# A graph layer on one core: counts of a block made in pairs of pairs, and five searches of the opening moved back

## The chip, the cores and the metric

The kernel runs on one core of a Trainium2 chip. The metric is the device time of one execution in microseconds, as the median of the runs shown. The profile is of one further execution, whose own time stands beside its span below.

## The reference

A layer of a graph network over 6250 nodes with 64 features and 206,250 edges. The edges are sorted by their destination; half of the random edges are the other half reversed, and each node has a loop to itself.

```
h   = relu(layernorm(x))                        # 6250 x 64
msg = h[src] + edge_attr_64                     # 206250 x 64
agg = segment_sum(msg, dst)                     # 6250 x 64
out = x + relu(agg @ W1 + b1) @ W2 + b2         # hidden width 128
```

So each node sums over its edges the normalized features of the sources and the features of the edges, and two small dense layers follow.

## The kernel before

**Two sums.** The edge features are loaded in chunks of 42 nodes (SyncE's queue) and summed by TensorE with a one-hot matrix of the destinations, into a PSUM tile `bank` (`chunk_sum`, L517). The source features aren't gathered for most edges. Instead the kernel counts, for each destination, how often each source occurs, and multiplies the counts with the normalized features: sources are written as 49 rows h of 128, edges stand in tiles of 127 for 3 destinations each, and a tile's counts are one fp8 matmul of two one-hot matrices (`count`, L971; `hotb`, made by VectorE at L958). `count(n)` is called for odd steps n and makes 12 tiles (one pair of steps) in a PSUM tile `pc` of two buffers. ScalarE copies it into the SBUF `ring` (L981). For the last pair of a block that copy has two parts, the first 12 rows h ahead of the other 37. `products` (L994) then multiplies, for h = 0 to 48, the features of h with the ring's counts of a whole block of 252 nodes, into the PSUM tile `pv`.

**Blocks and steps.** There are 23 blocks (0 to 22) of 14 steps; a step is 6 tiles, so a block has 7 pairs, called below by their odd steps 1, 3, ... 13. The products of block b - 1 are run inside block b: 12, 12, 12 and 13 rows h at steps 1, 3, 5 and 7, each behind that step's count (`PART`, L86 and L1315). The ring holds 22 steps, so that the first 8 steps of block b have room beside the block before.

**What else stands in a block's order.** Feature sums at steps 9 and 11 (two and four of a block's six chunks, 48 and 96 matmuls as the trace counts them), the placing of the block before's feature sums into `pv` (L549) at step 3, at most two sums of an edge group (`sum_group`, L580, copied by ScalarE at L582) at steps 3 and 5, the first dense layer `ph` (L1072) at step 10 with its relu on ScalarE (L1074), the second `po` (L1080) at step 13, and the turning of the next edge keys (`pk`, L771, copied at L791 and L799). In blocks 7 to 14 a check `over` (`inside_rel`, L906) runs on ScalarE at step 8, ahead of that step's other work. `ph`, `po`, `over` and the values of the turned keys use one PSUM tile of one buffer, tag `po`.

**Who sets the order.** The order of the instructions of each engine is that of the program text. The loop over the steps (L1305) calls, for step n: what stands in `tops` and `before`, the count, the one-hot rows, the encoding of keys, the products, what stands in `later`, `turns` and `behind`. The lists `before` and `behind` are written by hand by step (L1182, L1205). GpSimd issues all indirect gathers, each at L360. The gathers of source rows for the last 17 edge groups go through a list `queue`, which `pool_until` works off by a clock of estimated costs; `room` limits how many gathers may be issued until a later step sets it again (L1105 to L1118).

**The opening.** Each of 15 rows of lists (row i covers 128 windows of 3 nodes) begins at an edge that has to be searched: `fetch_row(i)` gathers 256 destinations for each window on GpSimd, `seek(i)` counts on ScalarE with an accumulator how many are smaller (L383), and `place` turns this into an edge number on VectorE (L388, L390). The words of the lists are gathered at these numbers (`fetch_pair`). Also here, `chunk_starts` and `chunk_columns` work out where the feature chunks start, `fetch_dst(t)` gathers the destinations of 32 chunks (`dstq`), and the node features are normalized and split in two fp32r halves (L634, L638). Windows with more than 127 edges, at most 14, need a second list: `second_ends` to `second_nodes` find them (`pnext` at L831, ranks at L844 to L846, picks at L855 to L868) at the steps in `SECOND` (L84), ScalarE's and VectorE's parts by `before`, TensorE's by `behind`.

```
for n in range(NSTEP):
    b, s = block_of(n)
    for f in tops.get(n, []) + before.get(n, []):
        f()
    if n % 2:
        count(n)
    ...
    if b and 1 <= s < FRESH:
        products(b - 1, PART[s], PART[s + 1])
    ...
    for f in later.pop(n, []) + turns.pop(n, []) + behind.get(n, []):
        f()
    pair_ends(n)
```

Of the kernel before, what the change touches and what calls it, by code (L numbers as in the profile page):

```python
# [53 lines left out]
GA = G - GP  # L54
# [13 lines left out]
NW = 23  # L68
SB = 3
ST = 6  # L70
STEPS = BT // ST
# [9 lines left out]
UPPERS = (5, 7, 9)  # L81
LOWERS = (11, 15, 17)
CLEARS = (61, 47, 33, 19, 18)
SECOND = (7, 8, 9, 10, 11, 13, 14, 20, 22)  # L84
FIRST = 12
PART = (0, 0, 12, 12, 24, 24, 36, 36, HI)  # L86
CHUNKS = ((9, 9), (11, 11), (11, 11))
# [20 lines left out]
IC = -(-NWIN // P)  # L108
# [26 lines left out]
ROWS = 3  # L135
# [9 lines left out]
LAND_US = 4.0  # L145
NEED_P = N - 31 * GP - 6
OPENING_US = 8.0


def four_bytes(byte):  # L150
# [4 lines left out]
def gnn_kernel(ctx: ExitStack, tc: tile.TileContext, x, src_t, dst_t, dst_g, edge, w1, b1, w2, b2, out):  # L155
# [16 lines left out]
    def block_of(n):  # L172
        b = min(n // STEPS, NW - 1)
        return b, n - b * STEPS
# [200 lines left out]
    def fetch_row(i):  # L375
        at = rows_at + i * L1 if i < 11 else squares_at + (i - 11) * L1
        rows_of[i] = agg[:, at:at + L1].bitcast(I32)
        gather(rows_of[i], dst_g.rearrange("q h (r k) -> (q h r) k", k=L1), row_i[:, i:i + 1])

    def seek(i0, n):  # L380
        for i in range(i0, i0 + n):

            nc.scalar.activation(agg[:, junk_at:junk_at + L1 // 2].bitcast(BF16), rows_of[i], AF.Sign,  # L383
                                 bias=nhalf[:, i:i + 1], accum_out=first[:, i, 1:2])

    def place(i0, n):
        to = first[:, i0:i0 + n, 0]
        nc.vector.scalar_tensor_tensor(to, first[:, i0:i0 + n, 1], -0.5, middle[:, i0:i0 + n],  # L388
                                       op0=OP.mult, op1=OP.add)
        nc.vector.tensor_tensor(first_i[:, i0:i0 + n], to, limit[:, i0:i0 + n], op=OP.min)  # L390
# [56 lines left out]
    def fetch_dst(t):  # L447
        dsts[t] = late.tile([P, CQ], I32, tag="dstq", bufs=2, name="dstq")
        gather(dsts[t], dst_g.rearrange("q h (k o) -> (q h k) o", o=1), cols_i[:, t:t + 1])

    def chunk_nodes(t):

        dst = dsts.pop(t)
        relq = dst.bitcast(F32)
        nc.vector.tensor_scalar(relq, dst, cols[:, NT:], float(CN * RC * t), op0=OP.subtract, op1=OP.subtract)
        nc.vector.scalar_tensor_tensor(relq, iota_q, cols[:, t:t + 1], relq, op0=OP.subtract, op1=OP.max)
        known["n", t] = relq
# [94 lines left out]
    def tiles_of(g):  # L552
        return J if g < G - 1 else JL
# [56 lines left out]
    def norm_var(k):  # L610
        h0, h1 = thirds[k]
        nc.vector.tensor_reduce(var[:, h0:h1], squares.pop(k), AX.X, OP.add)  # L612
# [100 lines left out]
    def fetch_words(i0, n, p, index):  # L713
        words_of[i0] = late.tile([P, 2, P], I32, name="words", bufs=2)
        for i in range(n):
            gather(words_of[i0][:p, i, :], packed_1[:, :] if i0 < 4 else packed[:, :], index[i])

    def fetch_pair(i0):
        n = min(2, IC - i0)
        fetch_words(i0, n, P, [first_i[:, i:i + 1] for i in range(i0, i0 + n)])  # L720
# [166 lines left out]

    def second_fetch():
        queue.insert(0, (WORDS_US / 2, lambda: fetch_words(2 * PC, 1, NX, [flags.pop("i")[:, :]])))

    RP = 4
    bad = small.tile([P, 2 + 2 * RP], F32, name="bad")
# [202 lines left out]
    def fetch_h(g):  # L1095
        if g not in parts_of:
            load_h(g)
        for j in range(tiles_of(g)):
            queue.append((GATHER_US, lambda j=j: gather(
                parts_of[g][:, j, :], table[:, :], src_p[:, (g - GA) * J + j:(g - GA) * J + j + 1], OP.add)))  # L1100
        queue.append((0.0, lambda: fetched.setdefault(g, pool[0])))

    fetched = {}

    room = [1 << 30]  # L1105

    def pool_until(us):
        while queue and pool[0] <= us and (room[0] > 0 or not queue[0][0]):
# [16 lines left out]
            fetch_h(g + ROWS)  # L1125

    fetch_pair(0)
    for i in range(5, 11):
        fetch_row(i)
    seek(2, 1)  # L1130
    norm_var(0)
    for i in range(11, IC):
        fetch_row(i)
    src_turn(1)
    norm_var(1)
    firstp = small.tile([1, GP], F32, name="firstp")
# [24 lines left out]
    encode(0)  # L1161
    chunk_index(0, 2)
    fetch_dst(0)
    fetch_pair(2)
    fetch_dst(1)
    seek(7, 3)
# [4 lines left out]
    for q in range(2):  # L1171
        key_copies(1, q, columns(1))
    value_powers(1, columns(1))
    seek(10, 1)
    rows_of_tiles(1)
    load(0)
    for k in range(1, 3):
# [4 lines left out]
    load(2)  # L1182

    before = {
        2: [lambda: [fetch_h(g) for g in range(GA, GA + ROWS)], lambda: seek(11, 2)],
        5: [lambda: chunk_nodes(0), lambda: seek(13, 2)],
        6: [lambda: chunk_turn(0)],
        7: [lambda: place(7, 8)],
        18: [find_groups],
        87: [lambda: chunk_starts(2 * RC, NC)],  # L1190
        89: [lambda: chunk_rows(2 * RC, NC)],
# [10 lines left out]
    for n in range(2 * RP):  # L1202
        before.setdefault(106 + 14 * n, []).append(lambda n=n: inside_rel(n))

    behind = {}  # L1205
    for k in range(3):
        behind.setdefault(UPPERS[k], []).append(lambda k=k: split_upper(k))
        before.setdefault(LOWERS[k], []).append(lambda k=k: split_lower(k))
    for n, f in zip(SECOND, (second_ends, second_flags, second_ranks, second_picks, second_words, second_found, second_fetch, second_turn, second_nodes)):
        (behind if f in (second_ends, second_ranks, second_words, second_turn) else before).setdefault(n, []).append(f)  # L1210
# [24 lines left out]
    for i in range(2, IC):  # L1235
        c0, c1 = columns(i)[0][2], columns(i)[-1][2] + columns(i)[-1][1] - columns(i)[-1][0]
        n = min((n for n in range(deadline(c0) + 1 - TURN[-1][0]) if n % STEPS in (TURNS if i > 2 else (6,)) and c1 - R <= encoded(n)),
                key=lambda n: (i > 2 and TURNS.index(n % STEPS), -n))
# [4 lines left out]
            unpack_later(steps, lambda i=i: unpack_pair(i))  # L1243
        assert n <= (NW - 1) * STEPS + 7
        turn_later(n, i, P, columns(i))
    n = 27
    assert n + TURN[-1][0] <= deadline(SX)
    unpack_later([n - k for k in (4, 3, 2, 1)], lambda: unpack(2 * PC, 1, NX, second_b, NX))
    turn_later(n, 2 * PC, NX, [(0, NX, SX)])
    for t in range(1, NT):  # L1250
        n = 78 + 14 * t
        before.setdefault(n, []).append(lambda t=t: t > 1 and queue.insert(0, (GATHER_US, lambda: fetch_dst(t))))
        n = 49 if t == 1 else 86 + 14 * t
# [7 lines left out]
    for g in range(len(kept)):  # L1261
        n = 40 + 4 * g if g < 2 else 94 if kept[g][2] == 2 else XB * g * STEPS + 10
# [14 lines left out]
    for b in range(NW):  # L1277
        n = b * STEPS
# [23 lines left out]
        at_step(n, f)  # L1302

    assert len(PART) == FRESH + 1
    for n in range(NSTEP):  # L1305
        b, s = block_of(n)
        for f in tops.get(n, []) + before.get(n, []):
            f()
        if n % 2:
            count(n)  # L1310
        if n % (HT // ST) == 0:
            rows_of_tiles(n // (HT // ST) + 1)
        if n % (EB // ST) == AHEAD and n // (EB // ST) * EB + EB < TILES:
            encode(n // (EB // ST) + 1)
        if b and 1 <= s < FRESH:  # L1315
            products(b - 1, PART[s], PART[s + 1])
        if b and s == FRESH:
            add_products(b - 1)
            if b - 1 > SB:
                ready.append(b - 1)  # L1320
        if n in SECONDS:
            k = SECONDS.index(n)
            add_seconds(2 * k)
            if 2 * k + 2 >= NX:
                ready[:0] = range(SB + 1)
        if s in LAYERS and ready:
            mlp(ready.pop(0), n, LAYERS[s])
        for f in later.pop(n, []) + turns.pop(n, []) + behind.get(n, []):
            f()
        pair_ends(n)  # L1330
        if n >= 3:
            if s in (GROUPS if b < NW - 1 else LAST_GROUPS) and h_next < G and fetched.get(h_next, 1e9) + LAND_US <= clock(n + 2):
                group_hot(h_next)
                at_step(n + 2, features_h, h_next)
                h_next += 1
                add_later(n + 5)
            if n == 3:
                pool[0] = clock(n - 1) + OPENING_US
            pool_until(clock(n) + LAND_US)
# [5 lines left out]
    b = NW - 1  # L1345
# [161 lines left out]
```

## Time and profile before

| | before |
|---|---|
| median of 3 runs | 396.49 us (396.26 to 398.42) |
| the profiled execution | 396.92 us |
| its span, first to last instruction | 394.9 us |
| TensorE busy (matmul / weight load) | 335.2 us, 85% / 305.5 us, 77% |
| ScalarE busy | 327.0 us, 83% |
| VectorE busy | 307.5 us, 78% |
| GpSimd busy | 271.3 us, 69% |
| mean granted clock of TensorE | 0.995 of full speed |
| product runs (L994) | 1127 matmuls, 154.5 us |
| counts (L971) | 1932 matmuls, 78.3 us |
| copies into the ring (L981) | 184, 262.0 us |

The table is read so: no engine is busy all the time, and four are busy for more than two thirds of it, so a busy share alone doesn't say which one is waited for. That is read from the chain of waits and from the order of the instructions on TensorE and ScalarE in single blocks. TensorE's instructions overlap (a matmul's end is modelled), so the starts are the firmer numbers.

### The profile page before, as it was taken

To read this page: it belongs to the slowest core of one execution; us is meant where nothing else is said; L and a number is where in the kernel's file an instruction comes from. 1 tells how busy PE (TensorE), PEld (TensorE's weight loads), DVE (VectorE), ACT (ScalarE), POOL (GpSimd) and SP (SyncE) were. 2 spreads that over 40 slices of the span, in tenths; PEclk is the share of its full clock that TensorE was granted. 3 is DMA by queue.
4 is the path that set the end of the run, shared out by engine and by line. 5 is a ranking of instruction groups with operands and counts; after the bars stand their busy time and mean duration, and the time that the engine had idled before them with its cause. 6 is when DMAs were issued, how large, how long until landed. Compare 5 with 4: busy or idle time off the path is not lost.

```text
span 394.9 us, 17220 instructions
## 1 busy us (share of the span) xinstructions
PE 335.2 (85%) x7303; PEld 305.5 (77%) x7304; DVE 307.5 (78%) x804; ACT 327.0 (83%) x380; POOL 271.3 (69%) x204
## 2 busy tenths in 40 slices
PE   2053498889989989989899799989999999999993
PEld 1032387879878979979799799979889889988983
DVE  5965799989996977858886878978886878696631
ACT  7673979799989778978898989988889889987750
POOL 7774688877876885758767676767765876676400
PEclk9999999999999999999999999999999999999997
DMA  8967975869795785967868769967968976787500
GB/s 174 266 225 233 298 195 130 240 176 230 181 266 124 204 208 129 275 186 180 235 167 230 214 154 229 257 172 176 260 149 223 254 204 150 204 219 188 150 11 24
DMA packets 111947, 76.89 MB, mean 195 GB/s; under 512 B 30855, under 2 KB 107775, under 8 KB 111865
## 3 DMA queue, kind: packets, MB, share of 16 engines
q1 hardware_dynamic: 91134, 67.20, 57.0%
q0 software_dynamic: 20560, 8.28, 15.9%
q8 instruction: 59, 0.97, 1.0%
q10 hardware_dynamic: 171, 0.26, 0.2%
q14 instruction: 23, 0.19, 0.2%
HBM read 71.45 MB, written 4.26 MB: 192 GB/s over the span
## 4 chain that ended last, share of the span: by engine, by line
PE 71%; ACT 12%; DVE 6%; issue 5%; another core or an unknown queue 2%; DMA 1%; POOL 0%; DVEq 0%; ACTq 0%; SPq 0%; POOLq 0%
PE pv L994 31%; PE bank L517 13%; PE pc L971 13%; ACT ring L981 8%; PE ph L1072 3%; PE po L1080 3%; PE pv L549 3%; PE bank L580 2%; PE pk L771 2%; DMA xl<-in_x 1%; ACT sums L643 1%; DVE sums L601 1%; DVE sums L612 1%; ACT kq L791 1%
## 5 line engine op out<-in xcount | busy, mean ns | idle before, releaser
L981 ACT ACTIVATE ring<-pc 128x1764 fp32r<-128x1764 uint8 (+3 forms) x184 | 262.0, 1476 | 28.1 <-PE pc L971 18.0
L360 POOL DMA_INDIRECT pfeat<-table,src_p x132 | 226.2, 1713 | 78.2 <-PE bank L517 43.8
L994 PE MATMUL pv<-ring,h 128*128 128x252 f32 x1127 | 154.5, 286 | 10.2 <-ACT ring L981 9.0
L994 PEld LDWEIGHTS pv<-ring,h 128*128 128x128 f32 x1127 | 137.2, 188 | 12.5 <-ACT ring L981 10.6
L958 DVE TENSOR_TENSOR hotb<-at,of 127x576 int32<-127x576 bf16 x216 | 120.1, 599 | 2.0 <-PE pc L971 0.8
L971 PE MATMUL pc<-hotb 128*128 128x49 fp8e5 x1932 | 78.3, 186 | 4.3 <-issue 2.1
L971 PEld LDWEIGHTS <-hotb 128*128 128x128 fp8e5 x1932 | 67.7, 98 | 14.6 <-issue 4.2
L517 PE MATMUL bank<-feat,hotf 128*18 128x64 f32 x3288 | 64.5, 222 | 3.5 <-issue 2.8
L517 PEld LDWEIGHTS bank<-feat,hotf 128*18 128x18 f32 x3288 | 51.6, 99 | 10.1 <-issue 7.2
L504 DVE TENSOR_TENSOR hotf<-rel,iota 128x432 f32<-128x432 bf16 x69 | 41.5, 601 | 5.9 <-PE ph L1072 2.0
L1029 DVE TENSOR_TENSOR sums<-sums,pv 128x252 f32<-128x252 f32 (+2 forms) x27 | 8.1, 328 | 24.4 <-PE pv L994 19.3
L941 DVE TENSOR_TENSOR at<-iota_a,kq 128x576 bf16<-128x576 bf16 (+1 forms) x54 | 24.2, 448 | 0.4
L791 ACT ACTIVATE kq<-pk 128x512 bf16<-128x512 f32 (+18 forms) x48 | 17.9, 458 | 6.5 <-remote 5.0
L360 POOL DMA_INDIRECT words<-packed,first_i x15 | 17.1, 1143 | 5.6 <-issue 4.0
L947 DVE TENSOR_TENSOR of<-of,kv 128x288 bf16<-128x288 bf16 (+1 forms) x54 | 16.6, 308 | 2.6 <-ACT kv L799 0.2
L1072 PE MATMUL ph<-sums,w1s 128*128 128x252 f32 (+2 forms) x48 | 16.1, 416 | 2.9 <-ACT over L906 1.5
L360 POOL DMA_INDIRECT sums<-in_dst_g,row_i x15 | 15.0, 1001 | 4.8 <-issue 4.3
L306 PE MATMUL psrc<-shift,src 128*64 128x128 f32 (+1 forms) x16 | 4.1, 433 | 16.8 <-ACT src L303 16.8
L941 DVE TENSOR_TENSOR of<-iota_w,kq 128x288 bf16<-128x288 bf16 (+1 forms) x54 | 16.2, 300 | 0.6 <-ACT kq L791 0.6
L306 PEld LDWEIGHTS psrc<-shift,src 128*64 128x64 f32 (+1 forms) x16 | 3.1, 243 | 16.7 <-ACT src L303 12.1
L1080 PE MATMUL po<-w2s,after 128*126 128x64 f32 (+2 forms) x96 | 15.2, 280 | 0.0
L527 DVE COPY after<-bank 128x384 f32<-128x384 f32 (+1 forms) x23 | 12.7, 551 | 2.7 <-PE pc L971 2.7
(190 smaller groups left out, 300.5 us busy)
## 6 DMA issues: line engine op xcount, KB each, us to landing
feat<-in_edge SPq DMA_DIRECT2D x137, 384.0 KB
pfeat<-in_edge SPq DMA_DIRECT2D x16, 256.0 KB
pfeat<-table,src_p POOLq DMA_INDIRECT x132
xl<-in_x SPq DMA_DIRECT2D x3, 512.0 KB
out_y<-after SPq DMA_DIRECT2D x22, 63.0 KB
table<-xl SPq DMA_DIRECT2D x2, 512.0 KB
after<-in_x SPq DMA_DIRECT2D x4, 252.0 KB
table<-xl SPq DMA_DIRECT2D x1, 544.0 KB
```

The costliest lines, as they stand in the source:

```text
L360: ins = nc.gpsimd.indirect_dma_start(out=rows, out_offset=None, in_=source, in_offset=bass.IndirectOffsetOnAxis(ap=index, axis=0), compute ...
L504: nc.vector.tensor_tensor(hot_of[u][:, :n].rearrange("p c j w -> p (c j) w"), rel[:, c:c + n].rearrange("p c q k -> p (c q k)").unsqueeze( ...
L517: ins = nc.tensor.matmul(bank[q * QP:q * QP + WQ, at:at + D], hot_of[u][:, c, j, :], feats[u][c][:, j, :], start=(k == 0), stop=(k == JP - 1))
L791: nc.scalar.activation(kq[:, q, at:at + n].rearrange("s i k o -> s (i k) o"), pk[:, q, a:a + n].rearrange("s i k -> s (i k)").unsqueeze(2) ...
L941: nc.vector.tensor_tensor(to[:, :n].rearrange("s i k (m o) -> s (i k) m o", o=2), iota_k.rearrange("s (m o) -> s m o", o=2).unsqueeze(1).t ...
L947: nc.vector.tensor_tensor(pairs_of, pairs_of, kv[:, c:c + n].rearrange("s i k o -> s (i k) o").unsqueeze(2) .to_broadcast([P, 2 * n, WE // ...
L958: nc.vector.tensor_tensor(hot[:SLOTS, :n, c:c + m * A8].rearrange("s i (w a) -> s i w a", a=A8), at[:SLOTS, o:o + n, k].unsqueeze(2).to_br ...
L971: nc.tensor.matmul(pc[:, j * WPC:j * WPC + HI], hot[:, :P], hot[:, P:P + HI], start=True, stop=True)
L981: done.append(nc.scalar.activation(to[:, h:z, :mid - u], of[:, h:z, u:mid, :V], AF.Copy))
L994: nc.tensor.matmul(pvs[b], h2[:, h, :], ring[:, h, c:c + columns_of_block(b)], start=(h == 0), stop=(h == HI - 1))
L1072: nc.tensor.matmul(ph[:, :n], w1s, agg[:, start[b]:start[b + 1]], start=True, stop=True)
L1080: nc.tensor.matmul(po[:pairs[b], k, :], hid[:, k:2 * pairs[b]:2], w2s, start=True, stop=True)
```

## The change

Three things. First, in blocks 1 to 21 the counts of pairs 1 and 3 are both made at step 3, those of 5 and 7 at step 7, those of 9 and 11 at step 11, and that of 13 at 13 (`counted_at`); in the first and the last block each stays at its own step. Second, `fetch_row` of 10 to 14 goes on GpSimd behind `fetch_dst(0)`; `seek` of 10 to 14 goes behind steps 5 to 9, one each; `place(7, 8)` goes from step 7 to step 10, and the steps of the second lists' search in `SECOND` follow, with the unpacking and turning of the second lists' words from step 27 to 28. Third, `room` starts at 5 and not without a limit; `second_fetch`, at step 14, lifts the limit.

```diff
@@ -81,7 +81,7 @@
 UPPERS = (5, 7, 9)
 LOWERS = (11, 15, 17)
 CLEARS = (61, 47, 33, 19, 18)
-SECOND = (7, 8, 9, 10, 11, 13, 14, 20, 22)
+SECOND = (10, 11, 11, 12, 12, 14, 14, 20, 22)
 FIRST = 12
 PART = (0, 0, 12, 12, 24, 24, 36, 36, HI)
 CHUNKS = ((9, 9), (11, 11), (11, 11))
@@ -145,6 +145,7 @@
 LAND_US = 4.0
 NEED_P = N - 31 * GP - 6
 OPENING_US = 8.0
+OPENING = 5
 
 
 def four_bytes(byte):
@@ -887,6 +888,7 @@
 
     def second_fetch():
         queue.insert(0, (WORDS_US / 2, lambda: fetch_words(2 * PC, 1, NX, [flags.pop("i")[:, :]])))
+        room[0] = 1 << 30
 
     RP = 4
     bad = small.tile([P, 2 + 2 * RP], F32, name="bad")
@@ -1102,7 +1104,7 @@
 
     fetched = {}
 
-    room = [1 << 30]
+    room = [OPENING]
 
     def pool_until(us):
         while queue and pool[0] <= us and (room[0] > 0 or not queue[0][0]):
@@ -1125,12 +1127,10 @@
             fetch_h(g + ROWS)
 
     fetch_pair(0)
-    for i in range(5, 11):
+    for i in range(5, 10):
         fetch_row(i)
     seek(2, 1)
     norm_var(0)
-    for i in range(11, IC):
-        fetch_row(i)
     src_turn(1)
     norm_var(1)
     firstp = small.tile([1, GP], F32, name="firstp")
@@ -1161,6 +1161,8 @@
     encode(0)
     chunk_index(0, 2)
     fetch_dst(0)
+    for i in range(10, IC):
+        fetch_row(i)
     fetch_pair(2)
     fetch_dst(1)
     seek(7, 3)
@@ -1171,7 +1173,6 @@
     for q in range(2):
         key_copies(1, q, columns(1))
     value_powers(1, columns(1))
-    seek(10, 1)
     rows_of_tiles(1)
     load(0)
     for k in range(1, 3):
@@ -1182,10 +1183,10 @@
     load(2)
 
     before = {
-        2: [lambda: [fetch_h(g) for g in range(GA, GA + ROWS)], lambda: seek(11, 2)],
-        5: [lambda: chunk_nodes(0), lambda: seek(13, 2)],
+        2: [lambda: [fetch_h(g) for g in range(GA, GA + ROWS)]],
+        5: [lambda: chunk_nodes(0)],
         6: [lambda: chunk_turn(0)],
-        7: [lambda: place(7, 8)],
+        10: [lambda: place(7, 8)],
         18: [find_groups],
         87: [lambda: chunk_starts(2 * RC, NC)],
         89: [lambda: chunk_rows(2 * RC, NC)],
@@ -1202,7 +1203,7 @@
     for n in range(2 * RP):
         before.setdefault(106 + 14 * n, []).append(lambda n=n: inside_rel(n))
 
-    behind = {}
+    behind = {n: [lambda i=n + 5: seek(i, 1)] for n in range(5, 10)}
     for k in range(3):
         behind.setdefault(UPPERS[k], []).append(lambda k=k: split_upper(k))
         before.setdefault(LOWERS[k], []).append(lambda k=k: split_lower(k))
@@ -1243,7 +1244,7 @@
             unpack_later(steps, lambda i=i: unpack_pair(i))
         assert n <= (NW - 1) * STEPS + 7
         turn_later(n, i, P, columns(i))
-    n = 27
+    n = 28
     assert n + TURN[-1][0] <= deadline(SX)
     unpack_later([n - k for k in (4, 3, 2, 1)], lambda: unpack(2 * PC, 1, NX, second_b, NX))
     turn_later(n, 2 * PC, NX, [(0, NX, SX)])
@@ -1302,12 +1303,19 @@
         at_step(n, f)
 
     assert len(PART) == FRESH + 1
+    def counted_at(n):
+        b, s = block_of(n)
+        if not 0 < b < NW - 1:
+            return [n] if n % 2 else []
+        return {3: [n - 2, n], 7: [n - 2, n], 11: [n - 2, n], 13: [n]}.get(s, [])
+
+    assert STEPS == 14
     for n in range(NSTEP):
         b, s = block_of(n)
         for f in tops.get(n, []) + before.get(n, []):
             f()
-        if n % 2:
-            count(n)
+        for k in counted_at(n):
+            count(k)
         if n % (HT // ST) == 0:
             rows_of_tiles(n // (HT // ST) + 1)
         if n % (EB // ST) == AHEAD and n // (EB // ST) * EB + EB < TILES:
```

## Rows read from the trace of the kernel before

**Rows 1.** The page's fourth part: the chain that ended last, its shares by engine.

```profile
PE 71%; ACT 12%; DVE 6%; issue 5%; another core or an unknown queue 2%; DMA 1%; POOL 0%; DVEq 0%; ACTq 0%; SPq 0%; POOLq 0%
```

**Rows 2.** Timeline, TensorE, 306.5 to 323: start, us, instructions xcount [idle before <-releaser].

```profile
308.44 1.66 PE L994 MATMUL pv<-ring,h 128*128 128x252 f32 x12 [0.88 <-ACT ring L981]
309.94 0.47 PE L971 MATMUL pc<-hotb 128*128 128x49 fp8e5 x12
...
317.78 0.69 PE L1072 MATMUL ph<-sums,w1s 128*128 128x252 f32 x2
...
322.65 0.61 PE L994 MATMUL pv<-ring,h 128*128 128x252 f32 x3 [0.16 <-issue]
```

**Rows 3.** Timeline, TensorE, three narrow windows behind 310.2, which part a run.

```profile
310.26 0.47 PE L994 MATMUL pv<-ring,h 128*128 128x252 f32 x2
...
310.46 0.51 PE L994 MATMUL pv<-ring,h 128*128 128x252 f32 x3
...
310.57 0.40 PE L994 MATMUL pv<-ring,h 128*128 128x252 f32 x2
```

**Rows 4.** Timeline, ScalarE, 304 to 324.

```profile
319.65 1.63 ACT L981 ACTIVATE ring<-pc 128x1764 fp32r<-128x1764 uint8 x1
322.06 1.71 ACT L981 ACTIVATE ring<-pc 128x432 fp32r<-128x432 uint8 x2 [0.78 <-PE po L1080]
```

**Rows 5.** Timeline, TensorE, 223.5 to 238.

```profile
223.65 1.66 PE L994 MATMUL pv<-ring,h 128*128 128x252 f32 x12 [0.66 <-ACT ring L981]
...
229.40 0.47 PE L971 MATMUL pc<-hotb 128*128 128x49 fp8e5 x12
...
232.52 0.69 PE L1072 MATMUL ph<-sums,w1s 128*128 128x252 f32 x2
```

**Rows 6.** Timeline, ScalarE, 222 to 239.

```profile
228.32 3.24 ACT L981 ACTIVATE ring<-pc 128x1764 fp32r<-128x1764 uint8 x2 [0.49 <-PE pc L971]
231.45 0.60 ACT L906 ACTIVATE over<-rel,edge_w 128x411 f32<-128x411 bf16 x1
231.98 0.19 ACT L906 ACTIVATION_READ_ACCUMULATOR over<-rel,edge_w 128x1 f32 x1
...
234.33 1.63 ACT L981 ACTIVATE ring<-pc 128x1764 fp32r<-128x1764 uint8 x1
```

**Rows 7.** Instructions of line L1072 (ph): its engine idle until (us, times).

```profile
  ACT over L906: 3.9, 6
```

**Rows 8.** Timeline, ScalarE, 24 to 60.

```profile
39.55 0.50 ACT L383 ACTIVATE sums<-sums,nhalf 128x256 bf16<-128x256 int32 x1
...
40.18 0.51 ACT L383 ACTIVATE sums<-sums,nhalf 128x256 bf16<-128x256 int32 x1
...
50.24 1.10 ACT L634 ACTIVATE h<-xl 128x1088 fp32r<-128x1088 f32 x1
```

**Rows 9.** Timeline, TensorE, 24 to 72.

```profile
47.16 0.58 PE L831 MATMUL pnext<-ends,shift 128*128 128x15 f32 x2 [1.23 <-DVE ends L829]
...
48.59 1.48 PE L517 MATMUL bank<-feat,hotf 128*18 128x64 f32 x48
...
55.16 1.67 PE L994 MATMUL pv<-ring,h 128*128 128x252 f32 x12 [0.65 <-ACT ring L981]
```

**Rows 10.** Timeline, GpSimd, 14 to 64.

```profile
30.52 0.95 POOL L360 DMA_INDIRECT sums<-in_dst_g,row_i  x1 [0.30 <-issue]
...
36.30 1.35 POOL L360 DMA_INDIRECT dstq<-in_dst_g,cols_i  x1 [4.83 <-DVE cols L442]
```

**Rows 11.** Windows: us, busy us of PE, PEld, DVE, ACT, POOL; clock, DMA share, GB/s.

```profile
27.00:32.00 5.00, 0.33 (x2) 0.00 (x0) 0.00 (x0) 1.48 (x6) 3.55 (x4) 1.00 1.00 360
```

**Rows 12.** Timeline, VectorE, 25 to 52.

```profile
33.52 0.21 DVE L414 TENSOR_SCALAR starts<-pstart 1x64 f32<-1x64 f32 x1 [6.64 <-remote]
...
46.84 0.17 DVE L829 TENSOR_SCALAR ends<-first 128x15 f32<-128x15 f32 x1
```

**Rows 13.** All waits: engine, what waited <- for what: us in total, times, longest.

```profile
PEld bank L517 <- issue: 7.2, 23, 0.6
```

## The prediction, made before the changed kernel was run

> **What bounds the kernel now.** I read the page first, for the chain that ended last. 71% of it is TensorE and 12% ScalarE [rows 1]: TensorE sets the pace, and ScalarE, which copies each pair's counts from PSUM into the ring, stands between two of its pieces. Then the timeline of TensorE over one block late in the run, from the first product run (h 0 to 11 of the block before) at 308.44 us to the next at 322.65, a period of 14.21 us [rows 2]. What to see there: TensorE works without a break except in front of that first run, which waits 0.88 us for ScalarE's copy. Third, ScalarE in the same block [rows 4]: it has idle time, 0.78 us of it in front of the first part of the last pair's copy (322.06), which starts 4.28 us behind the MLP's ph (317.78) and releases the product run 0.59 us later. So one block is TensorE's work, plus one trip over ScalarE, whose slack is under 1 us. Fourth, a block in the middle, from 223.65 [rows 5, 6]: a check copy named over runs on ScalarE behind the copy of the fourth pair and shares a PSUM tile with ph; 6 idle times of ph's weight load or matmul, 3.9 us together, were ended by it [rows 7]; there are 8 such blocks (7 to 14). Last the opening up to 55.16 us, where the first product run starts [rows 8 to 12].
>
> **The counts, plain blocks.** I call a pair by its odd step. Counts 1, 5 and 9 move behind 3, 7 and 11; nothing is added or taken away. A count run takes 0.32 us (309.94 to 310.26) [rows 2, 3]. Behind it a product run's second matmul comes 0.20 us after the first (310.26 to 310.46), the next 0.11 after that (310.57) [rows 3]: a switch from counts to products costs 0.09 us. Up to ph: count 1, which filled the wait in front of the first run and so cost nothing, now costs 0.32 beside count 3; joining 5 and 7 saves a switch, 0.09; count 9 leaves, 0.32 + 0.09. Sum -0.18 us: ph comes earlier. Behind ph it is worse. Copy 11 starts 1.87 us behind ph in this block (319.65) [rows 2, 4] and 1.81 in the other (232.52 to 234.33) [rows 5, 6]; with the change copy 9 stands there and copy 11 comes behind it. Two copies in a row take 3.24 us (228.32) [rows 6], so one is 1.6 or a little less, 1.52 with the overlap. The last pair's copy starts at 1.75 + 1.52 + 1.52 = 4.79 us behind ph, where 4.28 is now: +0.51. Net +0.33 us a block, 13 blocks, +4.3 us. Bounds: -0.18 (ScalarE's slack larger than this block shows) and +0.5.
>
> One rule speaks against pairs here. The wait in front of the product run repeats in nearly every block, and its releaser is ScalarE's copy, a datum and not a free buffer [rows 2]. The Trainium skill (Perfetto Trace Analysis, Optimization Strategy) says that a gap which repeats on the saturated engine can mean too little PSUM for the next tile. By that rule a pair, which takes both count buffers, would wait as well. The trace does not yet bear it out: it is a rival below.
>
> **The blocks with the check copy.** Counts 5 and 7 now both follow the third product run, which ended at 229.40 [rows 5]; count 1 adds 0.32 before it, count 5 takes 0.32 and a switch away, so it ends at about 229.3, count 5 at 229.6. The two copies need 3.24 us: 232.9, where now they end at 231.45 [rows 6]. over, from its start at 231.45 to the end of its accumulator at 232.17 [rows 6], takes 0.72: 233.6, ph then, not 232.52: +1.1 us, and behind it the +0.51 from above. That is at most 1.6 us a block; where ph waits for something else as well it is 0.3 to 0.5. I take 0.9 for 8 blocks, +7.2 us, nearer the middle because at most six of the eight now wait for over at all [rows 7]. Bounds 2.4 and 12.8.
>
> **The opening.** Five row gathers, 0.95 + 0.30 us each [rows 10], go behind the first gather of destinations. That gather itself gains nothing on POOL: it waited 4.83 us for its index from VectorE. Behind the moved gathers stand two gathers of words, the second of destinations and the first features, all some 6.3 us later; the words are needed tens of us later and POOL has idle time then, so I cost this at nothing; without that cover the first feature groups would be late by the 6.3 us. SP's queue issues the same loads in the same order. The five searches (0.63 us apart, 39.55 to 40.18) [rows 8] go behind steps 5 to 9; ScalarE has the same work in all, so the last one ends about where the last upper split starts now, 50.24 [rows 8]. VectorE's place and ends wait for it, then TensorE's pnext. Ends and the way to TensorE take 0.32 (46.84 to 47.16) [rows 9, 12], and place's two short operations I put at as much: pnext comes at 50.9 and not at 47.16, 3.7 later. TensorE is in order, so the eleventh step's count, the second feature sums, the ranks and the picks queue behind it; the first sums (48.59, 1.48 us) [rows 9] now go ahead with a count run of 0.32: 1.8. The first product run at 55.16 moves by 3.7 - 1.8 = 1.9, and by the picks, which no feature sum hides any more: five short VectorE operations at 0.17 like ends, 0.9 with the way between. That is 2.8. Against that, less DMA: from 27 to 32 us the DMA engines are full [rows 11] and VectorE waits 6.64 us until 33.52 [rows 12] for a releaser that the profile does not name. Five gathers of 128 KB at 360 GB/s are 1.8 us of it; I take 0.5, as most of their packets could not run there anyway, with 0 and 6.64 as ends. Net +2.3. The limit of five feature gathers lets the second lists' words go first; at 5 gathers for 8 it costs nothing while their group comes later. The unpacking of those words, one step later, has VectorE's idle time around it, and the turn behind it moves by that step alone: nothing.
>
> Next to the row: the Trainium skill (DMA: Bandwidth & Descriptors, Queues, rings and completion order) says that each DMA engine serves its queues in turn, packet by packet. By it the five gathers share the full stretch, and leaving it gives up to 1.8 us; the sum would be 1.3 us lower.
>
> **Sum.** 4.3 + 7.2 + 2.3 = 13.8. Longer blocks give feature loads more time: the feature sums' weight loads sat 7.2 us in 23 unexplained stops [rows 13]; I let 40% of it go, -2.9. +10.9 us on the profiled execution's own 396.92 (span 394.9 and 2.0 around it) is 407.8; the median of the runs, 396.49, is 0.43 lower: 407.4, said as 407.
>
> **Rivals.**
> *Faster by the switches.* If ScalarE's slack covers the late copies (in plain blocks it idles before 322.06 [rows 4]) and ph does not wait, what is left is -0.18 us a block, or 21 x 0.18 = 3.8 us: 392.7. It decides where the copy of pair 7 ends before the feature sums in front of ph do. For it: 12% of the chain only is ScalarE [rows 1]. Against: the 6 waits of ph for over [rows 7]. Chance 0.13.
> *Faster by the opening.* The 6.64 us wait hangs on the DMA traffic that the moved gathers add, and shrinks by several us; with the pairs neutral some 391. Against: the gathers are few beside the 5 us at full load [rows 11, 12]. Chance 0.11.
> *No change.* Gain and loss cancel, or blocks were held by loads: 396.5. Chance 0.11.
> *Much slower.* A pair of counts takes both count buffers at once, so its second count waits until the copy of the count two before has ended; half a copy (0.8 us) a block in 21 blocks is 17 more: 424, or a good part of it. Against: the later copy of the earlier pair ends before the next pair is due in both blocks worked out. Chance 0.05.
> *Forecast, slower by late copies:* 0.60.
>
> **How the numbers follow.** The likeliest case gives 407, and its own range, from the bounds of its terms, 399 to 413. A measurement of this kernel can tell about 0.5%, 2 us, from no change. Slower by more: 0.60 + 0.05 = 0.65; same 0.11; faster 0.13 + 0.11 = 0.24. The range 393 to 413 leaves out most of the faster cases and the far slow one, about 0.2.
>
> **What would show it.** Right: in blocks 1 to 21 two copies in a row start behind the third product run and behind ph; ph in blocks 7 to 14 starts about 1 us later and is released by over; the wait of the first product run for ScalarE grows; the first product run starts at about 57.5 us. Wrong: ph no later in those blocks, a period of 14.0 us in the plain ones, or VectorE's wait until 33.52 gone.

## The result, and the profile after

The changed kernel takes 419.1 us (median of 6 runs, 416.76 to 423.38) beside 396.87 for the kernel before on the same chip: a ratio of 1.0546 (95% interval 1.0502 to 1.059), or 22 us more. I forecast 407. The direction was right; the size was under half of what was measured, and the time lies above the range's upper end of 413.

The profiled execution took 423.38 us, the longest of the six, at a mean granted clock of 0.972, while the shortest, 416.76, had 0.990. So the parts below add up to the loss of that execution, 26.5 us, and not to the 22 of the medians.

Where the time went, by the starts of the first product runs of the blocks (before / after, profiled executions): the first one starts at 55.16 / 55.95 us, the twenty-second at 365.02 / 391.68, and behind that both take 30 us more. So +0.8 us lie in the opening and +25.9 in the 21 blocks between: +14.9 in blocks 7 to 14, which have the check copy, and +11.0 in the other thirteen.

The chain that ended last (page, fourth part), by engine; ScalarE has 19% where it had 12% [rows 1]:

```profile
PE 65%; ACT 19%; issue 6%; DMA 4%; DVE 2%; POOL 1%; ACTq 0%; DVEq 0%
```

**A plain block.** Timeline of TensorE, then of ScalarE, of the changed kernel in a late block (answers to [rows 2, 4]; start, us, instructions, idle time ahead and what ended it):

```profile
362.31 1.66 PE L996 MATMUL pv<-ring,h 128*128 128x252 f32 x12 [0.56 <-ACT ring L983]
...
371.87 0.69 PE L1074 MATMUL ph<-sums,w1s 128*128 128x252 f32 x2
372.40 0.76 PE L973 MATMUL pc<-hotb 128*128 128x49 fp8e5 x24
...
377.14 1.08 PE L996 MATMUL pv<-ring,h 128*128 128x252 f32 x7 [1.00 <-ACT ring L983]
```

```profile
372.68 0.47 ACT L1076 ACTIVATE after<-ph,b1s 128x252 f32<-128x252 f32 x1 [0.22 <-PE ph L1074]
373.50 4.77 ACT L983 ACTIVATE ring<-pc 128x1764 fp32r<-128x1764 uint8 x4 [0.35 <-PE pc L973]
```

Here is what was forecast: copies 9 and 11 and both parts of 13 stand in one row behind ph. The copies begin 1.63 us behind ph, and the product run 5.27 behind it, where it was 4.87 [rows 2].

**A block with the check copy** (TensorE, then ScalarE, of block 14; answers to [rows 5, 6]):

```profile
276.34 0.77 PE L973 MATMUL pc<-hotb 128*128 128x49 fp8e5 x24
...
281.45 1.13 PE L1074 MATMUL ph<-sums,w1s 128*128 128x252 f32 x2 [1.94 <-ACT over L908]
```

```profile
277.61 3.17 ACT L983 ACTIVATE ring<-pc 128x1764 fp32r<-128x1764 uint8 x2 [1.98 <-PE pc L973]
280.67 0.61 ACT L908 ACTIVATE over<-rel,edge_w 128x411 f32<-128x411 bf16 x1
```

ScalarE stands idle for 1.98 us, then makes both copies and over in a row, and ph waits for over. Over the run (what line L1074's engines sat idle for; it was 3.9 us, 6 times [rows 7]; each wait stands here twice, for the weight load and for the matmul, and TensorE's matmuls alone waited 11.6 us in seven blocks, where it was 1.5 in two):

```profile
  ACT over L908: 24.4, 14
```

**The clock.** Windows of two stretches of 4 us with the start of a block's products in each; the column behind the five engines is the granted clock:

```profile
332.00:336.00 4.00, 4.00 (x42) 3.91 (x42) 3.83 (x12) 2.50 (x3) 3.39 (x3) 0.60 0.98 267
362.30:366.30 4.00, 3.99 (x52) 3.81 (x54) 3.44 (x9) 3.81 (x5) 3.39 (x3) 1.00 1.09 304
```

In the first, TensorE had the lower of its two clocks (1.2 GHz, half) for most of the stretch. There are six such stretches in the blocks of the changed kernel, near 104, 135, 183, 234, 282 and 333 us, and none in the blocks of the kernel before on this chip.

**The opening** (VectorE's starts and TensorE's pnext and first product run; answers to [rows 12] and [rows 9]):

```profile
27.86 0.20 DVE L415 TENSOR_SCALAR starts<-pstart 1x64 f32<-1x64 f32 x1
```

```profile
48.90 0.58 PE L832 MATMUL pnext<-ends,shift 128*128 128x15 f32 x2 [4.30 <-DVE ends L830]
...
55.95 2.93 PE L996 MATMUL pv<-ring,h 128*128 128x252 f32 x12 [0.62 <-ACT ring L983]
```

The wait of 6.64 us until 33.52 is gone, and TensorE waits 4.30 us in front of pnext instead.

### The profile page after: what moved, and what is told of

Read it like the earlier page. It is cut to its first block, busy times and chain, and to the rows that moved or that the text cites. A ratio compares the mean times of both kernels' runs of the same rounds, so it can differ in the third digit from the quotient of the medians.

```text
span 421.5 us, 17242 instructions
## 1 busy us (share of the span) xinstructions
PE 341.8 (81%) x7303; PEld 310.5 (74%) x7304; DVE 308.0 (73%) x804; ACT 328.7 (78%) x380; POOL 270.3 (64%) x204
## 4 chain that ended last, share of the span: by engine, by line
PE 65%; ACT 19%; issue 6%; DMA 4%; DVE 2%; POOL 1%; ACTq 0%; DVEq 0%
PE pv L996 33%; ACT ring L983 15%; PE pc L973 12%; PE bank L518 7%; DMA sums<-in_dst_g,row_i 4%; PE ph L1074 4%; PE pv L550 3%; PE bank L581 2%; ACT sums L384 1%; PE po L1082 1%; ACT over L908 1%; PE pw L779 1%; ACT after L1076 1%; PE pk L772 1%; PE pdst L464 1%
## 5 line engine op out<-in xcount | busy, mean ns | idle before, releaser
L983 ACT ACTIVATE ring<-pc 128x1764 fp32r<-128x1764 uint8 (+3 forms) x184 | 256.4, 1458 | 44.8 <-PE pc L973 41.8
L361 POOL DMA_INDIRECT pfeat<-table,src_p x132 | 222.7, 1687 | 102.5 <-PE bank L518 70.6
L996 PE MATMUL pv<-ring,h 128*128 128x252 f32 x1127 | 159.1, 292 | 17.4 <-ACT ring L983 17.3
L996 PEld LDWEIGHTS pv<-ring,h 128*128 128x128 f32 x1127 | 141.2, 193 | 23.1 <-ACT ring L983 22.1
L960 DVE TENSOR_TENSOR hotb<-at,of 127x576 int32<-127x576 bf16 x216 | 120.5, 600 | 16.2 <-PE pc L973 13.2
L973 PEld LDWEIGHTS <-hotb 128*128 128x128 fp8e5 x1932 | 64.0, 99 | 18.2 <-issue 9.8
L973 PE MATMUL pc<-hotb 128*128 128x49 fp8e5 x1932 | 69.3, 187 | 9.8 <-ACT ring L983 4.9
L518 PE MATMUL bank<-feat,hotf 128*18 128x64 f32 x3288 | 63.2, 229 | 3.2 <-DVE hotf L505 1.7
L1074 PE MATMUL ph<-sums,w1s 128*128 128x252 f32 (+2 forms) x48 | 17.0, 437 | 12.5 <-ACT over L908 11.6
L1076 ACT ACTIVATE after<-ph,b1s 128x252 f32<-128x252 f32 (+2 forms) x24 | 11.3, 470 | 17.2 <-PE ph L1074 13.6
L361 POOL DMA_INDIRECT sums<-in_dst_g,row_i x15 | 16.6, 1106 | 4.8 <-issue 4.0
L1074 PEld LDWEIGHTS ph<-sums,w1s 128*128 128x128 f32 x48 | 7.4, 194 | 15.0 <-ACT over L908 12.8
```

The costliest lines, as they stand in the source:

```text
L361: ins = nc.gpsimd.indirect_dma_start(out=rows, out_offset=None, in_=source, in_offset=bass.IndirectOffsetOnAxis(ap=index, axis=0), compute ...
L518: ins = nc.tensor.matmul(bank[q * QP:q * QP + WQ, at:at + D], hot_of[u][:, c, j, :], feats[u][c][:, j, :], start=(k == 0), stop=(k == JP - 1))
L960: nc.vector.tensor_tensor(hot[:SLOTS, :n, c:c + m * A8].rearrange("s i (w a) -> s i w a", a=A8), at[:SLOTS, o:o + n, k].unsqueeze(2).to_br ...
L973: nc.tensor.matmul(pc[:, j * WPC:j * WPC + HI], hot[:, :P], hot[:, P:P + HI], start=True, stop=True)
L983: done.append(nc.scalar.activation(to[:, h:z, :mid - u], of[:, h:z, u:mid, :V], AF.Copy))
L996: nc.tensor.matmul(pvs[b], h2[:, h, :], ring[:, h, c:c + columns_of_block(b)], start=(h == 0), stop=(h == HI - 1))
```

## The experiments

They ran on three other chips, on which the kernel before takes 377.2 to 377.6 us and not 396.9. So each is given against the kernel before on its own chip. The times in some expectations are still those of the first chip; what is compared is the difference. Traces of the three are set side by side, since the kernel before is alike on them, but not with the first. A block's time in them is read as above, from one first product run to the next. Theory A was that of the prediction, with the clock added: joined counts make ScalarE's copies late.

**1. The joined counts alone.** The first part of the diff (`counted_at` and its call) on the kernel before.

> The kernel before with the joined counts alone; opening, searches and limit of gathers as before. Theory A (the joined counts make all of the loss: two copies in a row hold ph in blocks 7 to 14 and the product run in every block, and TensorE's clock falls to half behind the longer waits): 417 to 423 us, ph waits for over some 11 us in 7 or 8 blocks, some dips of the granted clock to 0.5. Rival B (the opening and the limit of five gathers make a good part of the loss): 403 to 410.

Measured: 405.53 us against 377.53, ratio 1.071 (1.0651 to 1.0769). The counts alone make +28.0 us, the whole loss and more than the 20 to 26 that the expected times stand above the first chip's. Theory A; rival B falls. The trace has four falls of the clock to half in the blocks, so that part of the theory holds in kind.

**2. The opening alone.**

```diff
-        return {3: [n - 2, n], 7: [n - 2, n], 11: [n - 2, n], 13: [n]}.get(s, [])
+        return [n] if n % 2 else []
```

> The changed kernel with each count at its own step again, so the moved row gathers and searches and the limit of five gathers alone. Theory A: 396 to 398 us, first product run at about 56 us, no dip of the clock in the blocks. Rival B: 405 or more, feature groups late for want of gathers.

Measured: 376.4 us against 377.53, ratio 0.9974 (0.9941 to 1.0007): no difference that can be told. Moved searches, later second lists and the limit of five gathers together cost nothing; experiment 9 shows that this is a sum of a gain and a loss.

**3. The check copy earlier.**

```diff
-        before.setdefault(106 + 14 * n, []).append(lambda n=n: inside_rel(n))
+        before.setdefault(103 + 14 * n, []).append(lambda n=n: inside_rel(n))
```

> The changed kernel with the check copy over of blocks 7 to 14 at step 5 and not 8, ahead of the copies of pairs 5 and 7. Theory A (ph waits because over stands behind both copies): ph no longer waits for over, 8 to 12 us come back, 408 to 411. Rival C (ph's wait is only where a lateness shows, which the next copies would give back anyway): 415 or more, and the wait moves to the product run.

Measured: 392.86 us against 377.53, ratio 1.0381 (1.0332 to 1.0431). Experiments 1 and 2 add up to 404.4 on this chip; so 11.5 us came back, at the upper end of theory A's 8 to 12. What ph's engines sat idle for:

```profile
  ACT over L908: 0.6, 2
```

The wait of ph is gone and did not reappear elsewhere: blocks 7 to 14 took 117.9 us together, and 128.7 with the joined counts alone. Rival C falls. The 11.5 us hold what the clock gave back as well, since the runs of experiment 1 had 0.975 to 0.983 and these have 0.991 to 0.997.

**4, 5, 6. One pair at a time.** The kernel before with a `counted_at` that joins 5 and 7 only, 9 and 11 only, or 1 and 3 only:

```diff
+        return {1: [n], 3: [n], 7: [n - 2, n], 9: [n], 11: [n], 13: [n]}.get(s, [])
...
+        return {1: [n], 3: [n], 5: [n], 7: [n], 11: [n - 2, n], 13: [n]}.get(s, [])
...
+        return {3: [n - 2, n], 5: [n], 7: [n], 9: [n], 11: [n], 13: [n]}.get(s, [])
```

> The kernel before with only pairs 5 and 7 joined (at step 7). Theory A: only the blocks with over lose, 1 to 1.3 us each: 404 to 408 us, and the wait of the product run behind a block is as before (about 0.5 us a block). Rival D (each joined pair costs the same, by the two count buffers): a third of the loss, 403 to 405, spread over all 21 blocks.

Measured: 390.84 us against 377.53, ratio 1.0357 (1.0307 to 1.0408): +13.3, where the expected times stand 8 to 12 above the first chip's. A miss in size, and in theory A's "only": blocks without over lose here too, as blocks 15 to 19 take 13.2 to 13.7 us where those of the kernel before (experiment 9) take 12.9 to 13.5, each 0.2 to 0.7 less. The profiled execution was the shortest of its five runs (385.25 to 392.66), so its rows don't carry the whole size.

> The kernel before with only pairs 9 and 11 joined (at step 11). Theory A (ScalarE has copies 9, 11 and the first part of 13 in a row behind ph, and the product run waits for the last): the largest of the plain blocks' losses, 0.5 to 0.7 us in each of 21 blocks, +10 to +15 us, ratio 1.027 to 1.04, the product run waits for ScalarE in most blocks, ph does not wait for over more than before. Rival D (each joined pair costs alike, by the count buffers): about +7, 1.02.

Measured: 390.96 us against 377.15, ratio 1.0362 (1.0246 to 1.0479): +13.8, as theory A expects. But the product run doesn't wait for ScalarE here: the count of pair 1 stands in front of it, as before, and it is this count that waits, for its buffer. All waits of that kernel (the longest, 1.7 us, lies in the opening), then ScalarE at the end of a block:

```profile
PE pc L971 <- ACT ring L981: 6.9, 12, 1.7
...
PE pv L994 <- ACT ring L981: 0.3, 1, 0.3
```

```profile
313.51 0.47 ACT L1074 ACTIVATE after<-ph,b1s 128x252 f32<-128x252 f32 x1 [1.44 <-PE ph L1072]
313.88 4.76 ACT L981 ACTIVATE ring<-pc 128x1764 fp32r<-128x1764 uint8 x4
```

ScalarE idles 1.44 us ahead of the relu, in the time in which copy 9 used to run, and has 4.76 us of copies behind it. The waits for the buffer, some 5 us in the blocks, don't make up the 13.8; where the rest goes is not shown.

> The kernel before with only pairs 1 and 3 joined (at step 3). Theory A: little, 0 to 0.2 us a block for the count that no longer fills the wait in front of the product run: 0 to +4 us, ratio 1.00 to 1.01. Rival D: about +7, 1.02.

Measured: 380.31 us against 377.15, ratio 1.0108 (1.0045 to 1.017): +3.2, theory A's size. The three pairs cost 13.3 + 13.8 + 3.2 = 30.3 us one by one and 28.0 together. With these intervals the sum is known to some 5 us, and within that the parts add; but pair 1 and 3 costs a quarter of the others, so rival D's equal thirds are not what is measured.

**7. The changed kernel on another chip.**

> The changed kernel itself, beside the others on one chip. If the parts add (joined counts +28.0, opening -1.1 on the earlier chip): ratio to the kernel before about 1.07. If the opening changes what the counts cost: under 1.06 or over 1.08.

Measured: 403.47 us against 377.15, ratio 1.072 (1.0611 to 1.0829), where the sum of experiments 1 and 2 is 1.071 and 0.997. The parts add.

**8. The opening with the second lists' search later still.** Experiment 2 with:

```diff
-SECOND = (10, 11, 11, 12, 12, 14, 14, 20, 22)
+SECOND = (13, 14, 14, 15, 16, 17, 17, 20, 22)
-OPENING = 5
+OPENING = 7
-        10: [lambda: place(7, 8)],
+        13: [lambda: place(7, 8)],
```

> The opening of the changed kernel, counts at their own steps, and the search of the second lists three steps later still (ends behind step 13, picks at 15, words at 16, their gather at 17; limit 7 gathers). Theory E (the opening gains 5 to 6 us where VectorE waited for the starts and gives them back where TensorE waits for ends in front of the eleventh count): no wait of pnext of several us, first product run 3 to 5 us earlier than with the changed opening, 371 to 374 where the kernel before has 377.5, ratio 0.985 to 0.99. Rival F (the blocks behind wait for loads and gathers, so an earlier start is given back): ratio 0.995 to 1.0.

Measured: 375.72 us against 377.15, ratio 0.9988 (0.9949 to 1.0027). The first product run came at 51.44 us, 3.5 earlier than in experiment 2 (54.92), as theory E expects, but nothing of that can be told in the time: rival F.

**9. The kernel before, for its trace on these chips.**

> The kernel before itself, for its trace on the chip of the other runs. Five other executions with its opening or the changed one had VectorE's starts at 26.9 to 28.9 us. Theory G (the wait until 33.52 of the first trace belonged to that execution or chip and not to the row gathers): starts at about 27 to 28 us, plain blocks of 12.9 to 13.1 us, the product run not waiting for ScalarE. Rival H (the gathers make the wait): starts at 33 us or later.

Measured: 378.18 us, a ratio of 1.0052 (1.0009 to 1.0095) to the other runs of the same kernel on this chip. So a ratio that differs from 1 by half a per cent means nothing here, whatever its interval. VectorE's starts came at 28.88: the kernel before has no wait of 6.64 us here, with all its row gathers where they were. Theory G, for these chips; whether the gathers have a part in the wait on the first chip stays open. The end of a plain block of this execution, TensorE and then ScalarE:

```profile
302.79 0.69 PE L1072 MATMUL ph<-sums,w1s 128*128 128x252 f32 x2
...
306.94 1.65 PE L994 MATMUL pv<-ring,h 128*128 128x252 f32 x12
```

```profile
302.16 1.64 ACT L981 ACTIVATE ring<-pc 128x1764 fp32r<-128x1764 uint8 x1 [0.33 <-PE pc L971]
303.70 0.47 ACT L1074 ACTIVATE after<-ph,b1s 128x252 f32<-128x252 f32 x1
304.05 1.64 ACT L981 ACTIVATE ring<-pc 128x1764 fp32r<-128x1764 uint8 x1
305.96 1.71 ACT L981 ACTIVATE ring<-pc 128x432 fp32r<-128x432 uint8 x2 [0.27 <-PE pc L971]
```

Copy 9 runs from 302.16, beside ph and up to the relu; the first part of copy 13 starts 3.17 us behind ph, and the product run waits for nothing. That is the place that the joined pair gives up.

The opening, too, can be read in this trace. Its first product run stands at 50.11 us, but its first block takes 20.21 us; in experiment 2 the run is at 54.92 and the block takes 14.49. The feature sums of that block wait, in the kernel before, for one-hot rows that VectorE makes late. VectorE itself waits ahead of them for the words of the second lists (TensorE, then VectorE):

```profile
67.53 1.49 PE L517 MATMUL bank<-feat,hotf 128*18 128x64 f32 x48 [5.24 <-DVE hotf L504]
```

```profile
64.90 0.27 DVE L741 TENSOR_SCALAR near<-words,second_b 14x128 int16<-14x128 int16 x1 [4.46 <-DMA words<-packed,second_i]
```

GpSimd gathers these words at 60.99 us, behind eight gathers of source features. In experiment 2, where the limit lets only five go ahead, it gathers them at 54.98; VectorE doesn't wait for them, and the same sums wait 0.28 us. So the limit does gain something, and the later searches lose about as much: the second block begins at 70.32 and 69.41. The gain differs between executions. With the opening of the kernel before, VectorE waits 2.1 to 2.9 us for the words in the traces of experiments 1, 6 and 7, 0.98 in that of 4, and not at all in that of 10 and on the first chip; with the limit it waits in none.

**10. The pair joined early.**

```diff
+        return {1: [n], 3: [n], 5: [n], 7: [n], 9: [n, n + 2], 13: [n]}.get(s, [])
```

> The kernel before with pair 11 made early, at step 9 behind pair 9, and not pair 9 late. As many joined pairs as with 9 and 11 at step 11. Theory A (what costs is that a copy starts later and ScalarE idles before it): 376 to 381 us, ratio 1.00 to 1.01, a count may wait some tenths for its buffer. Rival D (what costs is the joining, by the two count buffers or the release behind the second count): 388 to 392, ratio 1.03 to 1.04, as with the pair made late.

Measured: 383.19 us against 377.6, ratio 1.0166 (1.0109 to 1.0222): +5.6, between the two. Both expectations missed. The same pair joined late costs 13.8, so lateness is the larger part, and the joining by itself costs something. What that is stays open. Counts wait for their buffers:

```profile
PE pc L971 <- ACT ring L981: 5.5, 5, 2.8
```

But the longest of these waits, 2.8 us, lies in the opening, where nothing is joined, and the 2.7 us in the blocks stand beside 1.6 in the trace of experiment 9.

**11. TensorE's breaks filled.** In the changed kernel:

```diff
+        if 0 < b < NW - 1 and s == 13:
+            fill(n, 12)
         for k in counted_at(n):
             count(k)
+        if b > 1 and s == 1:
+            fill(n, 18)
```

with `fill` a row of matmuls of a one-hot tile into 44 unused columns of `bank`.

> The changed kernel with fp8 matmuls of no use (44 columns that nobody reads) where TensorE waits: 12 ahead of count 13 and 18 ahead of the first product run of blocks 2 to 22. Theory I (the granted clock falls to half because of TensorE's breaks at the end of a block): no stretch at 0.5 in the blocks, mean clock 0.995 or more in every run where the changed kernel has 0.972 to 0.99, and 2 to 6 us less than its 403: ratio 1.055 to 1.07. Rival J (the falls come whatever TensorE does there): clock 0.975 to 0.99 as before, time as the changed kernel or some us more.

Measured: 410.92 us against 377.6, ratio 1.0874 (1.0813 to 1.0934), clocks 0.973, 0.993, 0.998 and 0.993. The time went up. The added matmuls wait themselves, which may be a part of it:

```profile
PEld L1315 <- issue: 8.6, 9, 1.7
```

The clock was 0.993 or more in three of four runs, and the changed kernel never had over 0.990 in ten, on two other chips. The fourth, the profiled one, had 0.973: a long stretch at half clock in the opening (45.70 to 59.36 us), where nothing was added, and two short ones in blocks, as many as in the trace of experiment 7. The kernel before had 0.979 to 0.995 on this chip. So neither theory I nor J is settled by it, and the run gives no price.

**12. Both remedies.** Experiment 8 with over at step 5.

> Counts at their own steps, the changed opening with the search of the second lists three steps later, and over at step 5. Theory A: ph's waits for over (some 2.5 us) go too: 371 to 374 us, ratio 0.985 to 0.99. Rival F (the blocks wait for other things as well, so little of it shows): ratio 0.993 to 1.0.

Measured: 377.13 us against 377.6, ratio 0.9968 (0.9932 to 1.0003). Rival F: where ph waits only a little for over, the place of over is worth nothing that can be told; blocks 7 to 14 take 111.6 us here and 111.3 in experiment 8. No version here beats the kernel before clearly.

## Why the prediction was right in sign and wrong in size

**What held.** The path: the loss comes from the joined counts (experiments 1 and 2), through copies of ScalarE that start later. In the plain blocks from 15 on the term fits on the first chip: +0.33 us was forecast; six of the seven blocks were 0.33 to 0.65 longer (median 0.43) and one was 1.9 longer, the one in which the clock fell. ph to product run was forecast as 5.38 and measured as 5.27. There is luck in it. The 1.75 us in that sum stands in no row (1.87 and 1.81 do), and on the other chips the same blocks are 0.64 to 1.29 longer (experiment 7 against 9). Blocks 1 to 6 were 0.5 to 1.8 longer on the first chip (two falls of the clock lie there), so the thirteen plain blocks together cost 11.0 us and not 4.3.

The rival "much slower" came nearer in size, but its mechanism, counts that wait for their buffers, took 4.9 us in 8 places of the changed kernel (below; 1.3 of it in the opening) and not 17. The Trainium skill (Perfetto Trace Analysis, Optimization Strategy) says that a gap which repeats on the saturated engine can mean too little PSUM for the next tile; these rows agree in kind, and not in size.

```profile
PE pc L973 <- ACT ring L983: 4.9, 8, 1.3
```

**The step that failed most: the blocks with over.** The prediction put 0.9 us on each of 8, with 1.6 as the upper bound; they were 1.86 longer on the mean, +14.9 us and not +7.2. Three of the six stretches at half clock lie in them; without these some 10.5 us are left by the estimate below, or 1.3 a block. Two steps of the working were too small. First, it took 1.6 us down to 0.9 because at most six of eight blocks wait for over; those six are four weight loads and two matmuls, and with the change ph's matmul waits in seven of the eight. Second, it let the copies of 5 and 7 start at 229.6, with the end of count 5's run, 0.3 us behind its start, so that the way of a result to ScalarE cost nothing. In block 14 ScalarE starts them 1.27 us behind the start of the joined run (276.34 to 277.61), and ph is later by the difference. In the same block of experiment 7 (TensorE, then ScalarE) it takes 0.51 us:

```profile
265.31 0.77 PE L973 MATMUL pc<-hotb 128*128 128x49 fp8e5 x24
...
269.66 0.69 PE L1074 MATMUL ph<-sums,w1s 128*128 128x252 f32 x2 [1.18 <-ACT over L908]
```

```profile
265.82 3.17 ACT L983 ACTIVATE ring<-pc 128x1764 fp32r<-128x1764 uint8 x2 [1.21 <-PE pc L973]
```

Here the first copy starts while the joined run is still being issued (the product run behind it starts at 265.93), so it does not wait for the second count. In blocks 10 to 14 the wait of ph for over is 0.67 to 0.69 us longer than this way in both traces: 1.18 to 1.20 where the way is 0.51, and 1.18 to 2.05 on the first chip, where it is 0.51 to 1.36. Why results come later there stays open. That ph's wait is on the path is what experiment 3 shows.

**The term that was missing: the clock.** No sum or rival had TensorE at half clock. The two product runs and the counts between them take 336.91 - 331.73 = 5.18 us in the block at half clock, and 366.22 - 362.31 = 3.91 in the block shown above, which has a turn of values (0.18) more: 1.4 us a stretch, 8 to 9 us in the six of the profiled execution. That is an estimate from one pair of blocks. The runs agree in part: the shortest has a clock higher by 0.018 than the profiled one and is 6.6 us shorter, but a run at 0.974 took 419.15 us and one at 0.983 took 418.76. Some 20 us of the loss are there in the run that lost least to the clock. The trace of experiment 7 has two such stretches in its blocks and a loss of 26 us all the same.

That the falls come from the longer breaks is seen side by side, and not shown. Three of the six begin where ph waits 1.94 to 2.49 us for over, three behind breaks of 0.57 to 0.74 and 1.00 to 1.06 us at the end of a block; but breaks of 0.40 and 1.00 in front of 377.14 and one of 1.49 in front of 88.89 had no fall behind them, the kernel before falls too (at 66.29 us in the trace of experiment 9), and experiment 11 did not settle it. The Trainium skill (TensorE: Matmul & The Clock Gate, A second HAM failure mode: psum-queue depth-cycling) says of another kernel that frequent short idle times between groups of matmuls were enough to let the clock go up and down. The six falls among such waits agree with it in kind; the two of experiment 7, which has waits like them in nearly every block, show that such waits need not end in a fall.

**The opening.** Forecast +2.3, measured +0.8 at the first product run on the first chip, and on the whole no difference in experiment 2. The prediction took the wait of 6.64 us for a matter of the gathers' transfers, in part. On the other chips it does not exist in the kernel before (28.88), so it belonged to that execution or chip. Beside the rule that each DMA engine serves its queues in turn (the Trainium skill, DMA: Bandwidth & Descriptors, Queues, rings and completion order) the prediction gave the moved gathers up to 1.8 us; experiment 2 is 1.1 faster within an interval that holds 0, so no run here shows that gain. And it put the limit of five gathers at nothing, where experiment 9 shows the wait for the second lists' words that the limit takes away.

**Load waits.** The stops of the feature sums' weight loads went from 7.2 us to 3.0 (below), -4.2 where -2.9 was put. The matmuls behind them stood idle for less, 2.8 us and then 1.2, so the gain on TensorE was 1.6.

## What to carry to other kernels

Moving a producer's work later may cost nothing on its own engine and much on the consumer's: before two short pieces are joined, look for the idle time of the consumer that the first piece fills now, and for what stands behind the second. Price the consumer's start from the arrival of the result that the trace shows (here 0.5 to 1.4 us behind the start of the run), not from the end of the producer's run. And a stall that a single profile shows once in the opening should be seen in a second execution before a term is built on it.

## What was not expected of the hardware

The same kernel takes 396.9 us on the first chip and 377.2 to 377.6 on three others. Blocks 15 to 21 take 99.1 us together on the first chip and 91.8 in experiment 9, about 1 us each. Results of TensorE often reach ScalarE later on the first chip: the first part of the last pair's copy starts at 322.06 [rows 4], 1.58 us behind its count (320.48), and in the block of experiment 9 at 305.96, 0.78 behind it (305.18); ScalarE stood idle before both. The weight loads of the feature sums also stop for something that the profile doesn't name, 7.2 us in 23 places in the kernel before [rows 13], 3.0 in the changed kernel:

```profile
PEld bank L518 <- issue: 3.0, 8, 0.6
```

In experiment 7 it is 0.3 us, once, and in experiment 9 nothing; but experiment 10 has 6.3 us of such stops on the chip of experiment 9, so they are not the first chip's alone. Why the chip differs stays open.

The loss is smaller there (ratio 1.055, and 1.072 in experiment 7). The waits of the product runs for ScalarE show a part of the difference. On the first chip, kernel before and changed kernel:

```profile
PE pv L994 <- ACT ring L981: 9.0, 13, 1.0
```

```profile
PE pv L996 <- ACT ring L983: 17.3, 21, 1.5
```

The changed kernel in experiment 7, where in the kernel before (experiment 9) no matmul waits so:

```profile
PE pv L996 <- ACT ring L983: 14.0, 19, 1.5
```

So the copies were late on the first chip before the change, and the change adds 8.3 us there and 14.0 between experiments 9 and 7.
